# A cross-attention stream whose first chunk and queries are multiplied in unsplit fp32, with merged input transfers and unused products at the start

## The chip, the cores and the metric

The kernel runs on one core of a Trainium2 chip. The metric is the device time of one execution in microseconds. A core has five engines that run their own instruction queues and wait for each other through semaphores: TensorE (PE in the profile; its weight loads are PEld), VectorE (DVE), ScalarE (ACT), GpSimd (POOL) and SyncE (SP), which here issues the DMA transfers. All tiles lie in on-chip memory of 128 partitions; TensorE writes into accumulators (PSUM, here six banks of 128 x 512 for passing results and two that accumulate over the whole stream).

## The reference

The whole is one layer: cross-attention with a sigmoid in place of the softmax, then a causal attention block with rotary terms, then a mixture of 8 experts. What matters here is the first part. `x` has 256 rows of 512, the context 25088 rows of 512.

```
xn = layernorm(x)
qp = xn @ Wq.T + bq                  # 256 x 128
kp = ctx @ Wk.T + bk                 # 25088 x 128
vp = ctx @ Wv.T + bv                 # 25088 x 512
z  = sigmoid(qp @ kp.T / sqrt(128))  # 256 x 25088
x  = x + z @ vp
```

Then `x = x + attn(layernorm(x))` and `x = x + ffn(layernorm(x))`. All inputs are fp32.

## The kernel before

**Algebra and tiling.** The context is streamed once in 49 chunks of 512 keys. Each chunk comes twice from memory: transposed (`ctxT`, features on partitions, 1 MB) for the key product, and as it stands (`ctxN`, keys on partitions, 1 MB) for the weighted sum. The product with `Wv` is left to the tail: the stream accumulates `z @ ctx` in `acc[0]` and `acc[1]` (128 queries each) over all chunks, and the row sums of `z` in `zacc` for the bias.

**Split products.** A product of two fp32r tiles keeps fewer bits than one of plain fp32 tiles and takes less time (512 columns: 0.23 us from start to start at L88, against 0.87 us for the plain fp32 product at L522). To keep the bits all the same, an operand is split (`split`, L82): ACT casts it to fp32r (`hi`, L84), and DVE or POOL subtracts that from the source (`lo`, L85). `mm3` (L87) then issues three products, hi by hi, hi by lo and lo by hi (L88, L89, L90). In the tail, products that are few take both operands as plain fp32 in a single call.

**A chunk** `c` goes through these steps: `load_T` and `load_N` issue the transfers on SP; `split_T` and `split_N` split them; `kp_mm(c)` forms the keys (4 blocks of 3 products of 512 columns); `kp_out` adds the bias and splits the result (ACT L203, DVE L204); `scores` multiplies with `qp` (12 products of 256 columns a chunk), takes the sigmoid (ACT L212), adds `z` to `zacc` (DVE L214) and splits `z`; `av` accumulates (24 products of 512 columns). The loop at L288 works one chunk ahead: `kp_mm(c + 1)` stands ahead of the `av` products of chunk `c`, and `scores(c + 1, 0)` and `scores(c + 1, 1)` stand behind the `av` products of key tiles 1 and 2. The last two chunks' products for the second half of the queries are kept for the tail.

**The start** (L242 to L284) is what the change is about. SP issues, in this order, `wk` (256 KB), `x` in two halves, `wq`, chunk 0 of `ctxT` in four blocks, `bq` and `bk` as columns of 128 four-byte elements, chunk 1 of `ctxT` in two halves, chunks 0 and 1 of `ctxN`, and `bv`. ACT and POOL split `wk` and `wq`. DVE computes the moments of both halves of `x` (`moments`, L145, with the power -0.5 on POOL, L152) and normalizes (`normal`, L157). TensorE transposes the normalized halves (`transposed`, L162), and ACT and DVE split the transposed tile into `xh`, `xl`. Chunk 0 is split block by block, blocks 0 and 1 with DVE, 2 and 3 with POOL. TensorE's order is: two sets of transposes, `kp_mm(0)` blocks 0 and 1, the 12 products of the queries (L272), `kp_mm(0)` blocks 2 and 3, `kp_mm(1)` blocks 0 and 1, `scores(0, 0)`, `scores(0, 1)`, `kp_mm(1)` blocks 2 and 3, then the loop.

**What sets the order.** Each engine works through its instructions in the order in which the program issues them. Semaphores between engines follow from the tiles that are written and read; a tile of a tag with n buffers waits until the one n places before it is read to the end. DMA transfers share eight semaphores in turn, so a transfer may also wait for the one eight places before it. In the tail a written list (`ORDER`, L36) sets the order, step by step; step `N2v` (L654) writes the sum `x2` into the tiles in which `x` was.

Of the kernel before, what the change touches and what calls it, by code (L numbers as in the profile page):

```python
# [68 lines left out]
def body(ctx, tc, a, out, nch=NCH):  # L69
# [31 lines left out]
    def toks(t):  # L101
        return slice(t * P, (t + 1) * P)


    ident = sm.tile([P, P], F32, name="ident")
# [5 lines left out]
    x_sb = [sb.tile([P, D], F32, tag=f"x{t}", name=f"x_sb{t}") for t in range(2)]  # L111
    bq = sm.tile([P, 1], F32, name="bq")
    bk = sm.tile([P, 1], F32, name="bk")
# [92 lines left out]
    def scores(c, p):  # L206
# [7 lines left out]
        tt2(zacc, zacc, z, ALU.add)  # L214
        split(*zz[c, p], z)

# [20 lines left out]
    def load_split(n, tag):  # L237
        r = sb.tile([P, D], F32, tag="wr", name=f"{n}_r", bufs=2)
        nc.sync.dma_start(r, a[n])
        return r, pair(n, [P, D], tag)  # L240

    wk_r, wk = load_split("wk", "wk")  # L242
    for t in range(2):
        nc.sync.dma_start(x_sb[t], a["x"][:, t, :])
    wq_r, wq = load_split("wq", "at")
    load_T(0, 4)
    nc.sync.dma_start(bq, a["bq"])
    nc.sync.dma_start(bk, a["bk"])
    load_T(1, 2)
# [5 lines left out]
    xh, xl = pair("xa", [P, KD, T], "oh")  # L255
    warm = sm.tile([P, 1], F32, name="warm")
    nc.scalar.activation(warm, half, AF.Sigmoid)
    split(*wk, wk_r, nc.gpsimd)
    m = [moments(x_sb[tt], f"a{tt}") for tt in range(2)]
    xn = [normal(x_sb[tt], m[tt], f"xa{tt}") for tt in range(2)]  # L260
    split(*wq, wq_r, nc.gpsimd)
    xps = [transposed(bank(f"xa_ps{tt}"), xn[tt]) for tt in range(2)]
    for j in range(2):
        split_T(0, [j])
        split(xh[:, :, toks(j)], xl[:, :, toks(j)], xps[j])
    split_T(0, [2, 3], nc.gpsimd)
    load_T(2)
    kp_mm(0, [0, 1])
    qp = pair("qp", [P, T])
    ps = bank("qp_ps")[:, :T]  # L270
    for j in range(KD):
        mm3(ps, wq[0][:, toks(j)], wq[1][:, toks(j)], xh[:, j, :], xl[:, j, :], j == 0, j == KD - 1)  # L272
    kp_mm(0, [2, 3])
    split_T(1, [0, 1])
    split_T(1, [2, 3], nc.gpsimd)
    nc.scalar.activation(qp[0], ps, AF.Identity, bias=bq)
    nc.vector.scalar_tensor_tensor(qp[1], ps, bq, f(qp[0]), ALU.add, ALU.subtract)
    kp_out(0)
    split_N(0, [0, 1])
    kp_mm(1, [0, 1])  # L280
    scores(0, 0)
    scores(0, 1)
    split_N(0, [2, 3])
    kp_mm(1, [2, 3])  # L284

    per = -(-len(todo) // max(1, nch - 5))
    late = []
    for c in range(nch):  # L288
# [21 lines left out]
        if c < 2:  # L310
            split_N(c + 1)
        for t in range(NT):
            for q in now:
                av(c, t, q)
            if nx and t in (1, 2):
                scores(c + 1, t - 1)
# [8 lines left out]
    x2, xn, mo = [None] * 2, [None] * 2, [None] * 2  # L325
# [327 lines left out]
    @step  # L653
    def N2v(tt):  # L654
        x2[tt] = sb.tile([P, D], F32, tag=f"x{tt}", name=f"x2{tt}")
        tt2(x2[tt], ps_["wo", tt], x1[tt], ALU.add)
# [236 lines left out]
```

## Time and profile before

| what | value |
|---|---|
| three runs, median (lowest to highest) | 556.81 us (556.64 to 559.41) |
| profiled execution, its own time | 557.0 us |
| its span from the first to the last instruction | 555.2 us |
| busy share of the span: PE, DVE, ACT, POOL | 96%, 78%, 69%, 3% |
| mean granted clock of TensorE | 0.997 |
| data moved | 118.25 MB, mean 213 GB/s |

The page divides the span into 40 slices of 13.9 us. PE is at 9 tenths or more in nearly all of them; only the first slice (3 tenths) and the last one lie lower. A matmul's duration in the profile includes the time its result needs to come out, so that consecutive products overlap: what one costs in a run is the distance from start to start. A plain fp32 product appears as two records. Times are microseconds from the first instruction of the span.

### The profile page before, as it was taken

To read this page: it belongs to the slowest core of one execution; us is meant where nothing else is said; L and a number is where in the kernel's file an instruction comes from. 1 tells how busy PE (TensorE), PEld (TensorE's weight loads), DVE (VectorE), ACT (ScalarE), POOL (GpSimd) and SP (SyncE) were. 2 spreads that over 40 slices of the span, in tenths; PEclk is the share of its full clock that TensorE was granted. 3 is DMA by queue.
4 is the path that set the end of the run, shared out by engine and by line. 5 is a ranking of instruction groups with operands and counts; after the bars stand their busy time and mean duration, and the time that the engine had idled before them with its cause. 6 is when DMAs were issued, how large, how long until landed. Compare 5 with 4: busy or idle time off the path is not lost. (4 is left out here: it accounts for less than half of the span.)

```text
span 555.2 us, 7396 instructions
## 1 busy us (share of the span) xinstructions
PE 535.4 (96%) x2838; PEld 449.1 (81%) x2838; DVE 433.8 (78%) x471; ACT 381.4 (69%) x477; POOL 16.0 (3%) x25
## 2 busy tenths in 40 slices
PE   3999999999999999999999999999999999999984
PEld 3888888888888888888888888888888888887662
DVE  5899888887878787887878788787878788537853
ACT  5877787777676777667677777767677767528930
POOL 5200000000000000000000000000000000100000
PEclk9999999999999999999999999999999999999998
DMA  8997878774656647464655647475565747312001
GB/s 267 377 370 277 293 252 327 266 278 185 235 220 220 234 183 259 173 248 199 234 221 205 249 171 260 180 241 211 227 228 193 260 165 261 116 47 106 2 20 58
DMA packets 20644, 118.25 MB, mean 213 GB/s; under 512 B 2816, under 2 KB 3072, under 8 KB 7424
## 3 DMA queue, kind: packets, MB, share of 16 engines
q1 hardware_dynamic: 20608, 117.76, 58.6%
q8 instruction: 23, 0.38, 0.2%
q14 instruction: 13, 0.11, 0.0%
HBM read 115.13 MB, written 2.62 MB: 212 GB/s over the span
## 5 line engine op out<-in xcount | busy, mean ns | idle before, releaser
L85 DVE TENSOR_TENSOR N<-big,N 128x2048 fp32r<-128x2048 f32 (+1 forms) x53 | 112.1, 2119 | 57.7 <-ACT N L84 57.7
L88 PE MATMUL acc<-N,z 128*128 128x512 f32 x392 | 153.9, 393 | 0.0
L89 PE MATMUL acc<-N,z 128*128 128x512 f32 x392 | 153.7, 392 | 0.0
L90 PE MATMUL acc<-N,z 128*128 128x512 f32 x392 | 152.5, 389 | 0.0
L85 DVE TENSOR_TENSOR T<-big,T 128x2048 fp32r<-128x2048 f32 (+1 forms) x49 | 110.3, 2253 | 17.2 <-ACT T L84 17.2
L212 ACT ACTIVATE z<-sc 128x512 f32<-128x512 f32 x98 | 58.7, 599 | 78.8 <-PE sc L90 78.7
L84 ACT CAST N<-big 128x2048 fp32r<-128x2048 f32 (+1 forms) x55 | 94.4, 1725 | 6.2
L84 ACT CAST T<-big 128x2048 fp32r<-128x2048 f32 (+1 forms) x55 | 94.1, 1718 | 1.2 <-DMA big<-in_ctxT 1.2
L90 PEld LDWEIGHTS acc<-N,z 128*128 128x128 f32 x392 | 73.6, 188 | 16.1
L88 PEld LDWEIGHTS acc<-N,z 128*128 128x128 f32 x392 | 74.0, 189 | 12.3
L89 PEld LDWEIGHTS acc<-N,z 128*128 128x128 f32 x392 | 74.0, 189 | 11.7
L88 PE MATMUL kp_ps<-T,wk 128*128 128x512 f32 x196 | 76.9, 392 | 0.0
L90 PE MATMUL kp_ps<-T,wk 128*128 128x512 f32 x196 | 76.5, 390 | 0.0
L89 PE MATMUL kp_ps<-T,wk 128*128 128x512 f32 x192 | 74.7, 389 | 0.0
L214 DVE TENSOR_TENSOR zacc<-zacc,z 128x512 f32<-128x512 f32 x98 | 67.4, 688 | 6.9 <-ACT z L212 1.5
L85 DVE TENSOR_TENSOR z<-z,z 128x512 fp32r<-128x512 f32 x98 | 67.4, 688 | 0.0
L84 ACT CAST z<-z 128x512 fp32r<-128x512 f32 x98 | 61.0, 622 | 3.1
L203 ACT ACTIVATE kp<-kp_ps,bk 128x512 fp32r<-128x512 f32 x49 | 33.8, 691 | 39.8 <-PE kp_ps L90 39.8
L90 PE MATMUL sc<-qp,kp 128*128 128x256 f32 x196 | 55.8, 285 | 0.2 <-DVE kp L204 0.2
L89 PE MATMUL sc<-qp,kp 128*128 128x256 f32 x196 | 55.4, 283 | 0.0
L88 PE MATMUL sc<-qp,kp 128*128 128x256 f32 x196 | 54.9, 280 | 0.0
L88 PEld LDWEIGHTS kp_ps<-T,wk 128*128 128x128 f32 x196 | 37.1, 189 | 7.8
(174 smaller groups left out, 478.5 us busy)
## 6 DMA issues: line engine op xcount, KB each, us to landing
big<-in_ctxN SPq DMA_DIRECT2D x49, 1024.0 KB, 4.8
big<-in_ctxT SPq DMA_DIRECT2D x47, 1024.0 KB, 4.9
big<-in_gu SPq DMA_DIRECT2D x4, 1024.0 KB, 4.8
sp_wo<-w_wo SPq DMA_DIRECT2D x8, 256.0 KB, 4.4
wo<-sp_wo SPq DMA_DIRECT2D x2, 1024.0 KB, 6.1
big<-in_ctxT SPq DMA_DIRECT2D x4, 256.0 KB, 6.6
big<-in_ctxT SPq DMA_DIRECT2D x2, 512.0 KB, 6.3
r_wv<-in_wv SPq DMA_DIRECT2D x4, 256.0 KB, 6.6
```

The source lines that it names most:

```text
L84: copy(hi, src)
L85: eng.tensor_tensor(lo, src, f(hi), ALU.subtract)
L88: mm(ps, lhsT=ahi, rhs=bhi, start=first, stop=False)
L89: mm(ps, lhsT=ahi, rhs=blo, start=False, stop=False)
L90: mm(ps, lhsT=alo, rhs=bhi, start=False, stop=last)
L203: nc.scalar.activation(kp[c][0], ps, AF.Identity, bias=bk)
L212: nc.scalar.activation(z, ps, AF.Sigmoid, scale=1.0 / math.sqrt(128.0))
L214: tt2(zacc, zacc, z, ALU.add)
```

## The change

- `x` comes in one transfer into one tile of two halves; `x2` takes the same form in the tail.
- `bq` and `bk` come as two rows of 128 elements on ACT's queue, and two products with a one-element operand on TensorE turn them into two columns, which ACT copies from PSUM.
- Chunk 0 and chunk 1 of `ctxT` come in one transfer each; chunk 0 comes ahead of `wq`.
- Chunk 0 isn't split: `kp0(j)` multiplies `wk_r` with the arrived tile in plain fp32, four calls of 512 columns. The queries are formed from `wq_r` and the unsplit transposed `x` in four calls of 256 columns. `wq` is no longer split; `wk` still is, for the later chunks.
- `idle` issues products of a constant bf16 tile whose results nobody reads: five from the first microsecond on, and ten more behind the bias products.
- In the first chunks, more of the splits go to POOL, one block at a time; the order of the splits on ACT and DVE changes; `zacc` is added behind the split of `z` in chunk 0; and the scores of chunk 1 stand one key tile later among the products of chunk 0.

```
+    allb = sm.tile([P, P], BF16, name="allb")
+    nc.vector.memset(allb, 1.0)
...
-    x_sb = [sb.tile([P, D], F32, tag=f"x{t}", name=f"x_sb{t}") for t in range(2)]
-    bq = sm.tile([P, 1], F32, name="bq")
-    bk = sm.tile([P, 1], F32, name="bk")
+    x_all = sb.tile([P, 2, D], F32, tag="x", name="x_sb")
+    x_sb = [x_all[:, t, :] for t in range(2)]
+    brow = tmp("brow")[0:1, 0:2 * P].rearrange("p (i k) -> p i k", i=2)
+    bias = sm.tile([P, 2], F32, name="bias")
+    bq, bk = bias[:, 0:1], bias[:, 1:2]
...
-        tt2(zacc, zacc, z, ALU.add)
+        if c:
+            tt2(zacc, zacc, z, ALU.add)
         split(*zz[c, p], z)
+        if not c:
+            tt2(zacc, zacc, z, ALU.add)
...
-    def load_split(n, tag):
-        r = sb.tile([P, D], F32, tag="wr", name=f"{n}_r", bufs=2)
-        nc.sync.dma_start(r, a[n])
-        return r, pair(n, [P, D], tag)
-
-    wk_r, wk = load_split("wk", "wk")
-    for t in range(2):
-        nc.sync.dma_start(x_sb[t], a["x"][:, t, :])
-    wq_r, wq = load_split("wq", "at")
-    load_T(0, 4)
-    nc.sync.dma_start(bq, a["bq"])
-    nc.sync.dma_start(bk, a["bk"])
-    load_T(1, 2)
+    def idle(name, k):
+        ps = bank(name)
+        for _ in range(k):
+            mm(ps, lhsT=allb, rhs=allb[:, None, :].broadcast_to([P, 4, P]), start=True, stop=True)
+
+    wk_r, wq_r = (sb.tile([P, D], F32, tag="wr", name=f"{n}_r", bufs=2) for n in ("wk", "wq"))
+    nc.sync.dma_start(wk_r, a["wk"])
+    nc.sync.dma_start(x_all, a["x"])
+    load_T(0)
+    nc.sync.dma_start(wq_r, a["wq"])
+    for i, n in enumerate(("bq", "bk")):
+        nc.scalar.dma_start(brow[:, i, :], a[n].rearrange("p o -> o p"))
+    load_T(1)
     load_N(0)
     load_N(1)
     nc.sync.dma_start(bv, a["bv"])
...
-    xh, xl = pair("xa", [P, KD, T], "oh")
+    xa = sb.tile([P, KD, T], F32, tag="oh0", name="xa")
+    wk = pair("wk", [P, D])
     warm = sm.tile([P, 1], F32, name="warm")
     nc.scalar.activation(warm, half, AF.Sigmoid)
-    split(*wk, wk_r, nc.gpsimd)
+    idle("idlea", 5)
+    ps = bank("bias_ps")
+    for i in range(2):
+        mm(ps[:, i:i + 1], lhsT=brow[:, i, :], rhs=ones[0:1, :], start=True, stop=True)
+    copy(bias, ps[:, 0:2])
+    idle("idleb", 10)
+    kp[0] = bank("kp_ps0")
+
+    def kp0(j):
+        mm(kp[0], lhsT=wk_r[:, toks(j)], rhs=rT[0][:, j, :], start=j == 0, stop=j == KD - 1)
+
+    copy(wk[0], wk_r)
+    nc.gpsimd.tensor_tensor(wk[1], wk_r, f(wk[0]), ALU.subtract)
     m = [moments(x_sb[tt], f"a{tt}") for tt in range(2)]
     xn = [normal(x_sb[tt], m[tt], f"xa{tt}") for tt in range(2)]
-    split(*wq, wq_r, nc.gpsimd)
-    xps = [transposed(bank(f"xa_ps{tt}"), xn[tt]) for tt in range(2)]
-    for j in range(2):
-        split_T(0, [j])
-        split(xh[:, :, toks(j)], xl[:, :, toks(j)], xps[j])
-    split_T(0, [2, 3], nc.gpsimd)
+    xps = [transposed(bank("xa_ps0"), xn[0])]
+    kp0(0)
+    xps += [transposed(bank("xa_ps1"), xn[1])]
+    for j in range(1, KD):
+        kp0(j)
     load_T(2)
-    kp_mm(0, [0, 1])
+    copy(xa[:, :, toks(0)], xps[0])
+    vcopy(xa[:, :, toks(1)], xps[1])
+    split_T(1, [0, 1])
+    kp_out(0)
     qp = pair("qp", [P, T])
     ps = bank("qp_ps")[:, :T]
     for j in range(KD):
-        mm3(ps, wq[0][:, toks(j)], wq[1][:, toks(j)], xh[:, j, :], xl[:, j, :], j == 0, j == KD - 1)
-    kp_mm(0, [2, 3])
-    split_T(1, [0, 1])
-    split_T(1, [2, 3], nc.gpsimd)
+        mm(ps, lhsT=wq_r[:, toks(j)], rhs=xa[:, j, :], start=j == 0, stop=j == KD - 1)
+    split_T(1, [2])
+    kp_mm(1, [0, 1])
     nc.scalar.activation(qp[0], ps, AF.Identity, bias=bq)
     nc.vector.scalar_tensor_tensor(qp[1], ps, bq, f(qp[0]), ALU.add, ALU.subtract)
-    kp_out(0)
-    split_N(0, [0, 1])
-    kp_mm(1, [0, 1])
+    split_T(1, [3], nc.gpsimd)
+    split_N(0, [0])
+    split_N(0, [1], nc.gpsimd)
     scores(0, 0)
     scores(0, 1)
-    split_N(0, [2, 3])
     kp_mm(1, [2, 3])
+    split_N(0, [2])
+    split_N(0, [3], nc.gpsimd)
...
-        if c < 2:
-            split_N(c + 1)
+        if c == 0:
+            split_N(1, [0, 1])
+            split_N(1, [2, 3], nc.gpsimd)
+        if c == 1:
+            split_N(2)
         for t in range(NT):
             for q in now:
                 av(c, t, q)
-            if nx and t in (1, 2):
-                scores(c + 1, t - 1)
+            p = t - 1 - (c == 0)
+            if nx and p in (0, 1):
+                scores(c + 1, p)
...
-        x2[tt] = sb.tile([P, D], F32, tag=f"x{tt}", name=f"x2{tt}")
+        if tt == 0:
+            x2_all.append(sb.tile([P, 2, D], F32, tag="x", name="x2"))
+        x2[tt] = x2_all[0][:, tt, :]
```

More of the change, by code (lines that the diff above doesn't have):

```diff
@@ L324, in body @@
     x1 = [sb.tile([P, D], F32, name=f"x1{t}") for t in range(2)]
-    x2, xn, mo = [None] * 2, [None] * 2, [None] * 2
+    x2, xn, mo, x2_all = [None] * 2, [None] * 2, [None] * 2, []
     xT = [sb.tile([P, KD, P], F32, tag=f"xT{t}", name=f"xT{t}") for t in range(2)]
```

## The prediction

> **What bounds the kernel now.** I read four views: the page's busy rows, the table of busy time by stage, the order of time of the first 28 us, and the DMA issues. Stage table first; its columns are the stretch, its length, then busy us and count of PE, PEld, DVE, ACT and POOL, granted clock, DMA share, GB/s.
>
> ```profile
> PE 535.4 (96%) x2838; PEld 449.1 (81%) x2838; DVE 433.8 (78%) x471; ACT 381.4 (69%) x477; POOL 16.0 (3%) x25
> ...
> 0.00:7.63 7.63, 0.00 (x0) 0.00 (x1) 3.21 (x9) 2.36 (x4) 3.57 (x14) 1.00 0.73 199
> 7.63:15.73 8.10, 7.18 (x32) 6.03 (x33) 6.82 (x8) 6.16 (x12) 5.35 (x5) 1.00 0.96 367
> 15.73:27.49 11.76, 11.58 (x62) 9.71 (x60) 10.31 (x13) 10.88 (x15) 2.22 (x2) 1.00 0.90 370
> 27.49:461.31 433.82, 433.82 (x2162) 368.59 (x2160) 356.90 (x327) 312.62 (x325) 0.00 (x0) 1.00 0.65 235
> 461.31:555.20 93.89, 82.81 (x587) 64.81 (x585) 56.53 (x117) 49.42 (x124) 4.81 (x6) 0.98 0.22 79
> ```
>
> From 27.49, where chunk 2's key product starts, to 461.31 TensorE never rests: 45 chunks in 433.82 us, 9.64 each; DVE (82%), ACT (72%) and DMA (65%) have room. The diff touches nothing there that TensorE waits for, and the tail keeps its instructions. So the time changes by as much as the start of `kp_mm(2)` moves from 27.49, and everything is decided before it. There the order of time shows (start, duration, engine, line, what; in brackets the idle time and who ended it):
>
> ```profile
> 4.62 0.69 DVE L149 BATCH_NORM_STATS2 s6a<-x_sb 128x6 f32<-128x512 f32 x1 [3.01 <-DMA x_sb<-in_x]
> ...
> 6.02 0.69 DVE L149 BATCH_NORM_STATS2 s6a<-x_sb 128x6 f32<-128x512 f32 x1 [0.30 <-DMA x_sb<-in_x]
> ...
> 7.04 0.54 DVE L157 TENSOR_SCALAR xa<-x_sb,mva,rsa 128x512 f32<-128x512 f32 x1
> ...
> 7.63 1.12 PE L162 MATMUL xa_ps<-ident,xa 128*128 128x128 f32 x4 [7.63 <-DVE xa L157]
> ...
> 8.99 0.62 ACT L84 CAST T<-big 128x512 fp32r<-128x512 f32 x1 [1.01 <-DMA big<-in_ctxT]
> ...
> 11.43 0.63 PE L90 MATMUL kp_ps<-T,wk 128*128 128x512 f32 x1
> ...
> 11.86 0.63 PE L88 MATMUL kp_ps<-T,wk 128*128 128x512 f32 x1
> ...
> 13.71 1.15 ACT L84 CAST T<-big 128x512 fp32r<-128x512 f32 x2 [0.23 <-DMA big<-in_ctxT]
> ...
> 15.73 0.40 PE L88 MATMUL kp_ps<-T,wk 128*128 128x512 f32 x1
> ...
> 23.43 0.38 PE L90 MATMUL sc<-qp,kp 128*128 128x256 f32 x1 [0.18 <-DVE kp L204]
> ...
> 27.49 0.39 PE L88 MATMUL kp_ps<-T,wk 128*128 128x512 f32 x1
> ...
> 500.52 1.02 PE L522 MATMUL vs_ps<-wvu,ckv 128*128 128x512 f32 x2
> ```
>
> The reader is to see: x lands at 4.6 and 6.0, TensorE starts at 7.63 with transposes, and its products of 512 columns go every 0.43 us at 11.43 but every 0.2277 from 12.67 on (27.26 to 27.49). Chunk 1's first product goes at 15.73. From there to 27.49 stand 36 products of 512 columns (36 x 0.2277 = 8.20) and 24 of 256 (x 0.1175 = 2.82): 11.02 us of work in 11.76, so 0.74 us is stall, most of it at 23.43. The L522 row prices an unsplit fp32 product: two halves of 0.43 each, 0.87 for 512 columns; the eight products of 256 columns at L737 come every 0.43, and I use 0.44.
>
> **The change, part by part**, against the profiled execution: 557.0 us, 555.2 of span and 1.8 around it; 0.2 above the median of the three runs (556.81).
>
> *Transfers.* Before, pieces of 256 KB landed at 3.5 (wk), 4.6 and 6.0 (x), 7.3 (wq), 9.0, 9.6, 10.3, 11.0 (chunk 0), then chunk 1 at 13.7 and its values, 1 MB each, 2.5 us apart (16.2, 18.7). After, wk, x, chunk 0, wq, chunk 1 go in this order in whole pieces, and the 256 four-byte packets of bq and bk become two rows on ACT's queue. x: not before 3.5 + 1.27 (512 KB at the values' rate) = 4.7, not after 6.0, with as many bytes ahead as before; I take the middle, 5.4. Chunk 0: not before 4.7 + 2.5 = 7.2, not after 10.3, where as many bytes had landed; I take 8.5, nearer to the value row, since the 256 KB pieces from 9.0 on already came 0.65 apart. wq 9.6, chunk 1 at 12.1 (ends 10.5 and 13.6).
>
> [...]
>
> *Queries.* DVE's row for one half of x takes 1.10 us (4.62 to 5.72: statistics, aggregate, add), the second the same, and TensorE starts 0.6 after the first normalization starts (7.04 to 7.63): x + 1.1 + 1.0 + 0.6 = x + 2.7 = 8.1. That is 0.5 later than 7.63, since both halves now come together. The second half's normalization took 1.59 us beside POOL's split of wq; that split is gone, so it takes about 0.54 as the first did, done by 9.0.
>
> *TensorE to chunk 1.* Removed: 12 + 12 split products (12 x 0.2277 + 12 x 0.1175 = 4.1 warm, 1.2 more for the slow ones). Added: 4 x 0.87 + 4 x 0.44 = 5.2. With two sets of transposes (0.48 each by the late rows) it is 6.2 us in one run: 8.1 + 6.2 = 14.3 against 15.73, so the products that cost more pay by not waiting for splits. Chunk 0 is needed at 8.6; landing later than that, chunk 1 starts at landing + 5.7 (14.2 at 8.5).
>
> *Unused products.* Five from 1.3 on (0.43 each, to 3.5), then the two bias products, which wait for the bias rows, and ten more: 2.2 us at the fast pace, 4.3 at the slow. They end between 6 and 8.5 and push the transposes of 8.1 by 0 to 0.4; I take 0. The pace turned before 4.7 us after the first transposes (7.63 to about 12.4); counted from 1.3 that is 6.0, ahead of the queries. [...]
>
> *ACT, POOL, SP queues.* Two DMA issues (0.45 each by SP's rows) go ahead of ACT's table load, which ends at 3.0 instead of 2.0. Behind it wait the bias copy and wk's cast (4.6 instead of 3.49), then POOL's wk remainder (5.3 to 6.5) and, behind that on POOL, the power for x, ready at 6.5: nothing lost at x = 5.4, 0.3 at x = 4.7. SP has seven issues fewer ahead of the values, which only keeps its queue filled. Chunk 2's load waits for TensorE's last read of chunk 0 (12.5) instead of the splits (15.02) and lands near 20.4, before 21.9.
>
> *Splits of chunk 1.* After it lands: cast 0.61, two remainders 1.37, the remainder of kp 0.75, the third 0.69, that of qp 0.47: 3.9 us on DVE, so 16.0. The scores need it at 14.3 + 1.4 + 0.1 = 15.8: 0.2 to 0.3 lost. POOL takes three single pieces, 1.5 each by its rows (12.00, two in 2.99): ready at 17.0, 18.5, 21.7, used at 17.9, 19.8, 23.2; the cover is about 1 us each.
>
> *Scores of chunk 1 one tile later.* The remainder of kp is done at 22.0, the scores go at 22.6: the stall of 23.43 is gone. Next late is chunk 2's remainder on DVE, 24.9 against 25.6 needed. The zacc order and x's single tile cost nothing: same engine, same instructions, and in the tail the writer already stands behind the last reader.
>
> **Sum:** 14.3 + 0.3 + 11.0 = 25.6 for `kp_mm(2)`, 1.9 before 27.49; 557.0 - 1.9 = 555.1 us.
>
> **Rivals.**
> *Transfers no faster.* For it: all those bytes crossed by 10.3 and 13.6 before. Then chunk 1 starts at 10.3 + 5.7 = 16.0 and `kp_mm(2)` at 27.1: 556.6 us.
> *Transfers at full rate from wk on*, x at 4.4 to 4.7, chunk 0 by 7.2. For it: the value rows. Chunk 1 starts at 13.6, `kp_mm(2)` at 24.6: 554.1 us. Against it: DMA moved 199 GB/s in the first 7.63 us.
> *Pace not turned (the other side).* If the break for the bias rows, or TensorE's 1 us pause before the transposes, keeps the pace at 0.43, the 6.2 us cost up to 12.4: chunk 1 at 20.5, near 561 us. The change loses nothing until the pace turns after about 12.6 (chunk 1 at 16.6), and 0.5% only after about 18. Against it: in the rows of before, the pace turned with a pause of 0.92 us in between.
>
> **How the numbers follow.** Forecast (gains of 0.8 to 2.7) 0.53, transfers no faster 0.18, full rate 0.20, pace not turned 0.09. The 8 in 10 range cuts the outer part of the last two: 553.8 to 558.0. Half a per cent is 2.8 us, about what a measurement of this kernel tells from no change: faster by more, the full-rate case with what scatter adds, 0.20; slower by more, most of the pace case, 0.08; within, 0.72.
>
> **What would show it.** In the changed profile `kp_mm(2)` should start near 25.6, then 9.64 a chunk. Right steps: x ends DVE's wait at 5.4; chunk 0's fp32 products go 0.87 apart from 8.6; the first product of chunk 1 near 14.3; no gap near the scores of chunk 1. Wrong: fp32 products 1.7 apart; a DMA ending a wait of TensorE over 1 us; POOL's piece ending a TensorE wait after 17; a chunk period other than 9.64.

## The result and the profile after

| | before | after |
|---|---|---|
| median of 20 runs each (lowest to highest) | 558.84 us (556.64 to 561.47) | 558.09 us (557.07 to 560.97) |
| ratio after to before, 95% interval | | 0.9991, 0.9974 to 1.0008 |
| profiled execution, its own time; span | 557.0; 555.2 | 560.09; 558.3 |
| mean granted clock of TensorE in it | 0.997 | 0.989 |

The change makes no difference that can be measured. Before's three runs of the table above had a median of 556.81; its twenty have 558.84.

The table of busy time by stage, after (each row: stretch, length, then busy us and count of PE, PEld, DVE, ACT and POOL, granted clock, DMA share, GB/s):

```profile
0.00:7.75 7.75, 6.69 (x20) 2.89 (x21) 3.15 (x10) 2.16 (x4) 3.73 (x14) 1.00 0.73 258
7.75:14.27 6.52, 6.09 (x26) 3.74 (x24) 3.04 (x5) 2.92 (x5) 0.14 (x1) 1.00 1.00 419
14.27:26.92 12.65, 11.88 (x63) 9.61 (x62) 11.53 (x12) 11.08 (x18) 7.05 (x5) 1.00 0.91 350
26.92:461.06 434.14, 434.12 (x2162) 368.68 (x2161) 358.05 (x328) 313.15 (x325) 1.57 (x1) 1.00 0.65 234
461.06:558.30 97.24, 86.00 (x587) 66.58 (x585) 56.55 (x117) 49.36 (x124) 4.75 (x6) 0.94 0.21 76
```

Chunk 1 begins at 14.27, 1.46 earlier than before; chunk 2 (`kp_mm(2)`, the third stretch's end) at 26.92, only 0.57 earlier; chunk 4, at 46.54 against 46.79, only 0.25 earlier. POOL's busy time in the third stretch is 7.05 us; before it was 2.22 in the stretch from chunk 1 to chunk 2. The last stretch is 97.24 us long at a clock of 0.94, against 93.89 at 0.98. So the start gained 1.46, lost 1.2 of it again by chunk 4, and the tail, which the change leaves as it was, lost about 3 us in this execution. These are two matters, and both need their rows. (The trace's record of the granted clock begins only at 6.98; the unused products go 0.40 to 0.43 us apart ahead of it and 0.22 behind it, although the first row shows 1.00. In what follows, "the pace turns" means the beginning of that record.)

**The start**, in order of time (start, duration, engine, line, what; in brackets the idle time and who ended it):

```profile
1.06 2.31 PE L248 MATMUL idlea<-allb 128*128 128x512 bf16 x5 [1.06 <-DVE allb L106]
...
4.25 3.66 PE L248 MATMUL idleb<-allb 128*128 128x512 bf16 x10
4.92 0.69 DVE L153 BATCH_NORM_STATS2 s6a<-x_sb 128x6 f32<-128x512 f32 x1 [3.29 <-DMA x_sb<-in_x]
7.75 0.60 PE L166 MATMUL xa_ps<-ident,xa 128*128 128x128 f32 x4
8.78 1.10 PE L278 MATMUL kp_ps<-big,wk_r 128*128 128x512 f32 x2 [0.43 <-DMA big<-in_ctxT]
...
12.73 1.89 PE L297 MATMUL qp_ps<-xa,wq_r 128*128 128x256 f32 x8
14.27 0.59 PE L88 MATMUL kp_ps<-T,wk 128*128 128x512 f32 x1
...
22.83 0.50 PE L89 MATMUL acc<-N,z 128*128 128x512 f32 x1 [0.72 <-DVE N L85]
```

From the first unused product to 14.27 there is one wait, 0.43 us for chunk 0. The wait that matters is the last line: a product of values of chunk 0 (the chunk as it stands, `ctxN`) waits 0.72 us for the remainder of its block (`N`, the `lo` of the split, L85), and it is DVE that ends the wait, not POOL. From the start of the product before it that is 1.11 us instead of 0.23. A smaller wait of the same kind stands at 19.32, 0.44 instead of 0.23 behind the last start, for the remainder of `z`. Why DVE is late stands in its own rows beside POOL's, in the same view:

```profile
15.72 1.30 POOL L85 TENSOR_TENSOR T<-big,T 128x512 fp32r<-128x512 f32 x1 [7.83 <-ACT T L84]
...
16.19 1.37 DVE L85 TENSOR_TENSOR N<-big,N 128x512 fp32r<-128x512 f32 x1 [0.54 <-ACT N L84]
...
16.97 1.74 POOL L85 TENSOR_TENSOR N<-big,N 128x512 fp32r<-128x512 f32 x1
...
18.04 1.22 DVE L85 TENSOR_TENSOR z<-z,z 128x512 fp32r<-128x512 f32 x1 [0.47 <-ACT z L84]
...
20.28 1.35 POOL L85 TENSOR_TENSOR N<-big,N 128x512 fp32r<-128x512 f32 x1 [1.56 <-ACT N L84]
...
20.39 1.78 DVE L222 TENSOR_TENSOR zacc<-zacc,z 128x512 f32<-128x512 f32 x1
22.10 0.68 DVE L85 TENSOR_TENSOR N<-big,N 128x512 fp32r<-128x512 f32 x1
...
24.21 4.28 POOL L85 TENSOR_TENSOR N<-big,N 128x512 fp32r<-128x512 f32 x2 [2.59 <-ACT N L84]
...
25.56 3.48 DVE L85 TENSOR_TENSOR N<-big,N 128x512 fp32r<-128x512 f32 x2
```

A DVE subtraction or addition of 512 columns lasts 0.68 (the row at 22.10). Those that run while POOL works last 1.37, 1.22, 1.78. Add start and duration: POOL's pieces end at 17.02, 18.71 and 21.63; the DVE rows beside them end at 17.56, 19.26 and 22.17, each 0.54 or 0.55 later. So DVE's instruction doesn't seem to run more slowly all along; it seems to wait for POOL's to end. The waiting seems to go both ways: POOL's second piece, begun at 16.97 while DVE's row of 16.19 still ran, took 1.74 where the first took 1.30. At 24.21 POOL's two pieces end at 28.49 and DVE's second block at 29.04, 0.55 later again. So a piece that POOL takes from DVE is also taken out of DVE's time, and DVE is nearly full there (11.53 of 12.65 us in the third stretch).

The trace of before has the same pattern, in rows that the prediction read for another purpose or not at all:

```profile
8.02 1.59 DVE L157 TENSOR_SCALAR xa<-x_sb,mva,rsa 128x512 f32<-128x512 f32 x1 [0.45 <-POOL rsa L152]
...
8.06 1.27 POOL L85 TENSOR_TENSOR wq<-wq_r,wq 128x512 fp32r<-128x512 f32 x1
...
12.00 2.99 POOL L85 TENSOR_TENSOR N<-big,T 128x512 fp32r<-128x512 f32 x2 [2.67 <-ACT T L84]
...
12.99 2.55 DVE L85 TENSOR_TENSOR T<-big,T 128x512 fp32r<-128x512 f32 x2 [0.86 <-ACT T L84]
```

Two DVE blocks that take 1.28 together without POOL took 2.55 here and ended 0.55 after POOL's second piece (12.00 + 2.99 = 14.99; 12.99 + 2.55 = 15.54). The normalization of 8.02, of one tile and two columns, ended 0.28 after POOL's (9.61 against 9.33).

Not every DVE instruction is held. Before, POOL's next two pieces ran from 14.96 to 17.95. DVE's remainders of `qp` (15.46) and `kp` (16.65), which have one source in PSUM, took 0.47 and 0.75 beside them, and 0.48 and 0.74 in after with no POOL beside them (15.16 and 22.70). The next subtraction of two SBUF tiles, from 17.32, took 1.18 and ended at 18.50, 0.55 after POOL. Why the end lies 0.54 to 0.55 us behind POOL's, no trace or run here shows.

**The tail.** The same table of stages for the last 20 us, after:

```profile
538.12:542.87 4.75, 3.22 (x18) 2.40 (x17) 2.86 (x8) 0.86 (x2) 0.55 (x1) 1.00 0.08 30
542.87:549.70 6.83, 6.83 (x18) 4.08 (x18) 2.46 (x10) 0.00 (x0) 0.00 (x0) 0.50 0.21 77
549.70:553.11 3.41, 1.71 (x5) 0.43 (x3) 0.78 (x3) 0.54 (x2) 0.00 (x0) 1.00 0.00 0
553.11:558.30 5.19, 0.00 (x0) 0.00 (x0) 0.49 (x1) 0.00 (x0) 0.00 (x0) 0.50 0.17 58
```

and before, cut where its clock changed:

```profile
538.47:551.92 13.45, 8.56 (x37) 5.14 (x36) 6.58 (x21) 1.41 (x4) 0.55 (x1) 1.00 0.17 54
551.92:555.20 3.28, 0.00 (x0) 0.00 (x0) 0.00 (x0) 0.00 (x0) 0.00 (x0) 0.50 0.18 65
```

In after's execution the granted clock fell to 0.5 from 542.87 to 549.70, and TensorE's products there took nearly twice as long (the second gate and up products 3.62 us from 546.36, the first 1.99 from 538.12); in before's it fell only when TensorE had no more to do. That difference isn't the change's. In both kernels the runs lie in groups by mean granted clock: before, over the 106 runs that were taken beside the experiments, near 557.1 us at 0.997 to 0.998 (50 runs), 559 at 0.994 (22) and 561 at 0.990 (34); after, 557.8 (median of nine runs at 0.997) to 561.0. Taking the start of chunk 4 from the span in each profile makes the groups plain: from there to the end lie 508.4 us in before (555.23 - 46.79), and 508.4 to 508.7 in the eight other profiles in which the clock stayed full until the last products; 509.9 to 510.1 where the clock was at half for one step of 3.41 us; 511.5 to 511.8 where it was for two, as in after. So the time of a run is the start of chunk 4, plus 508.5, plus 0, 1.5 or 3.1 for the tail's clock, plus 1.8 around the span. For the rest of this document a kernel's start is read at chunk 4, and the tail apart.

### The profile page after: what moved, and what is told of

Its sections match the earlier page's. It is cut to its first block, busy times and chain, and to the rows that moved or that the text cites. A ratio compares the mean times of both kernels' runs of the same rounds, so it can differ in the third digit from the quotient of the medians.

```text
span 558.3 us, 7405 instructions
## 1 busy us (share of the span) xinstructions
PE 544.8 (98%) x2849; PEld 451.5 (81%) x2849; DVE 432.3 (77%) x469; ACT 378.7 (68%) x475; POOL 17.2 (3%) x25
## 5 line engine op out<-in xcount | busy, mean ns | idle before, releaser
L85 DVE TENSOR_TENSOR N<-big,N 128x2048 fp32r<-128x2048 f32 (+1 forms) x52 | 112.3, 2162 | 58.3 <-ACT N L84 58.3
L85 DVE TENSOR_TENSOR T<-big,T 128x2048 fp32r<-128x2048 f32 (+1 forms) x50 | 109.8, 2197 | 16.3 <-ACT T L84 16.2
L84 ACT CAST T<-big 128x2048 fp32r<-128x2048 f32 (+1 forms) x51 | 91.9, 1804 | 2.8 <-DMA big<-in_ctxT 2.8
L88 PE MATMUL kp_ps<-T,wk 128*128 128x512 f32 x192 | 74.9, 390 | 0.0
L90 PE MATMUL kp_ps<-T,wk 128*128 128x512 f32 x192 | 74.8, 390 | 0.0
L89 PE MATMUL kp_ps<-T,wk 128*128 128x512 f32 x192 | 74.8, 389 | 0.0
L219 DVE TENSOR_TENSOR zacc<-zacc,z 128x512 f32<-128x512 f32 x96 | 66.0, 688 | 6.8 <-ACT z L216 1.5
L85 DVE TENSOR_TENSOR z<-z,z 128x512 fp32r<-128x512 f32 x98 | 68.0, 694 | 0.5 <-ACT z L84 0.5
L207 ACT ACTIVATE kp<-kp_ps,bias 128x512 fp32r<-128x512 f32 x49 | 33.8, 690 | 38.4 <-PE kp_ps L90 38.4
```

Of the source, the lines that this page charges most:

```text
L84: copy(hi, src)
L85: eng.tensor_tensor(lo, src, f(hi), ALU.subtract)
L88: mm(ps, lhsT=ahi, rhs=bhi, start=first, stop=False)
L89: mm(ps, lhsT=ahi, rhs=blo, start=False, stop=False)
L90: mm(ps, lhsT=alo, rhs=bhi, start=False, stop=last)
L207: nc.scalar.activation(kp[c][0], ps, AF.Identity, bias=bk)
```

## The experiments

They were taken in four sets, each on one chip with the kernel before beside it; the medians of before were 557.61, 559.12, 558.43 and 559.08 in the four sets (29, 35, 29 and 13 runs). Nothing of the layer's computation is left out in any of them.

| kernel | chunk 1 starts | chunk 4 starts | from there to the end | median us (runs) | ratio to before, 95% |
|---|---|---|---|---|---|
| before | 15.73 | 46.79 | 508.4 | 558.84 (20) | |
| after | 14.27 | 46.54 | 511.8 | 558.09 (20) | 0.9974 to 1.0008 |
| values on DVE | 15.37 | 45.99 | 510.1 | 557.97 (12) | 0.9965 to 1.0015 |
| no unused products | 16.64 | 48.93 | 511.7 | 561.88 (6) | 1.0049 to 1.0098 |
| before, unused products | 14.85 | 46.71 | 511.5 | 557.97 (12) | 0.9970 to 1.0013 |
| before, tail filled | | 46.94 | 508.4 | 558.42 (12) | 0.9981 to 1.0022 |
| after, transfers cut | 14.37 | 46.64 | 508.4 | 557.41 (12) | 0.9950 to 0.9999 |
| cut, values on DVE | 13.65 | 45.57 | 509.9 | 557.14 (12) | 0.9939 to 0.9989 |
| the same, tail filled | 13.88 | 45.89 | 508.5 | 556.02 (12) | 0.9928 to 0.9972 |
| after, once more | 15.19 | 47.49 | 508.7 | 558.09 (12) | 0.9964 to 1.0011 |
| late values | 14.66 | 47.38 | 508.5 | 556.82 (12) | 0.9935 to 0.9981 |
| chunk 0 split | 13.82 | 44.80 | 508.5 | 555.42 (12) | 0.9915 to 0.9962 |
| late values, bias late | 13.56 | 48.64 | 508.5 | 556.92 (12) | 0.9942 to 0.9984 |
| chunk 0 split, bias late | 13.99 | 45.66 | 508.5 | 555.85 (10) | 0.9918 to 0.9967 |

The columns of starts are one execution each, the profiled one; medians are of all runs.

### Is it POOL? Values of chunks 0 and 1 on DVE

```
-    split_N(0, [1], nc.gpsimd)
+    split_N(0, [1])
...
-    split_N(0, [3], nc.gpsimd)
+    split_N(0, [3])
...
-            split_N(1, [2, 3], nc.gpsimd)
+            split_N(1, [2, 3])
```

> The changed kernel, with the six blocks of the values of chunks 0 and 1 that it gives to POOL subtracted on DVE instead. Contention theory: in the changed kernel DVE's rows of 0.69 us stretch to 1.2 to 1.8 while POOL subtracts, so the third block of chunk 0's values is ready at 22.78 and TensorE waits 0.72 there and 0.3 one chunk later. Without POOL these rows keep 0.69, the wait of 0.72 falls under 0.3, kp_mm(2) starts near 25.9 (26.92 in the changed kernel) and kp_mm(4) near 45.2 (46.54): 1.0 to 1.3 us less. Rival (DVE has no room for the added work): the six blocks add 4.1 us to DVE, the waits stay or grow, kp_mm(4) at 46.5 or later. Either way the tail keeps its scatter, so the time shows it only within about 1 us.

The edit moves four blocks, two of each chunk (the expectation says six). DVE has more instructions and each is short, in the order of time of that kernel:

```profile
19.19 0.68 DVE L85 TENSOR_TENSOR z<-z,z 128x512 fp32r<-128x512 f32 x1
...
20.99 0.68 DVE L222 TENSOR_TENSOR zacc<-zacc,z 128x512 f32<-128x512 f32 x1
21.59 1.28 DVE L85 TENSOR_TENSOR N<-big,N 128x512 fp32r<-128x512 f32 x2
...
25.92 2.49 DVE L85 TENSOR_TENSOR N<-big,N 128x512 fp32r<-128x512 f32 x4
```

Four blocks of chunk 1's values take 2.49 us; after, DVE's two took 3.48 beside POOL's two. From chunk 1's first product to `kp_mm(2)` it is 11.27 us instead of 12.65, with no wait of TensorE on DVE or POOL left in its rows from 9 to 38 us. The next chunk's period is 9.67. A late start of chunk 1 (15.37) isn't what makes these distances short: the second profile of the change (below) starts it at 15.19 and needs 12.63 and 10.03. The start of chunk 4 came only 0.55 earlier than after's, and not the 1.3 that was expected, since chunk 0 landed at 9.74 in this execution and TensorE waited 1.24 for it. In the median there is little (557.97 against 558.09); among runs of like clock there is more: the three at 0.997 took 555.1, 555.24 and 556.09 against a median of 557.81 for after and 557.16 for before beside it, and the four at 0.989 to 0.990 took 558.8 to 559.4 against 560.1 and 561.0 for after. POOL's share in the values is the cause of what was lost between chunk 1 and chunk 3, and the scatter that hides it lies elsewhere.

### Are the unused products needed? Without them, and before with them

```
-    idle("idlea", 5)
...
-    idle("idleb", 10)
```

> The changed kernel without its fifteen unused products. If they are what brings TensorE to its fast pace in time, then the fp32 products of chunk 0 go 1.7 us apart instead of 0.87 at least for the first, the pace turns between 11 and 15.6, the first product of chunk 1 starts at 15.5 to 17.3 instead of 14.27, and kp_mm(4) starts 0.5 to 2.5 later than 46.54, less where DVE is behind anyway. Rival (the pace turns through the transposes and fp32 products themselves): first product of chunk 1 within 0.3 of 14.27 and no change of kp_mm(4).

```profile
7.82 1.11 PE L166 MATMUL xa_ps<-ident,xa 128*128 128x128 f32 x4 [3.86 <-DVE xa L161]
9.66 2.04 PE L276 MATMUL kp_ps<-big,wk_r 128*128 128x512 f32 x2 [0.72 <-DMA big<-in_ctxT]
11.49 1.06 PE L166 MATMUL xa_ps<-ident,xa 128*128 128x128 f32 x4
```

The first unsplit product takes 2.04 here instead of 1.10, and the pace turns at 12.7. Chunk 4 starts at 48.93, 2.4 after the change with them (0.9 of it from a later landing of chunk 0), and the median is 561.88. This is the only one of the experiments that is measurably slower than before: without the unused products, the rest of the change costs more than it saves.

The same fifteen products put at the head of the kernel before, where the operands stay split:

```
+    allb = sm.tile([P, P], BF16, name="allb")
+    nc.vector.memset(allb, 1.0)
...
+    ips = bank("idlea")
+    for _ in range(15):
+        mm(ips, lhsT=allb, rhs=allb[:, None, :].broadcast_to([P, 4, P]), start=True, stop=True)
     split(*wk, wk_r, nc.gpsimd)
```

> The kernel before with fifteen unused products in front of its first transposes and nothing else of the change. Theory that the splits limit the start of before: the pace turns by about 7 instead of 12.6 and the first products go 0.23 apart, but chunk 0's last two blocks are subtracted on POOL until 15.0 (rows at 12.00, 2.99 for two), so the first product of chunk 1 comes no earlier than 15.4 (15.73 before) and kp_mm(4) moves by less than 0.4 from 46.79. Rival (the slow pace limits the start of before): six products at 0.43 become six at 0.23, 1.2 to 1.5 us less at kp_mm(4).

The pace turned at 4.0 and chunk 1 started at 14.85 instead of 15.73, but its second half started at 18.74 (18.75 before) and chunk 4 at 46.71 (46.79): the early start was lost again at the splits, where TensorE waited 0.5 us at 16.40. In before the pace isn't what limits; in after it is, as the two profiles of the change will show.

### Is the transfer's size worth something? Chunks 0 and 1 cut as before

```
-    load_T(0)
+    load_T(0, 4)
...
-    load_T(1)
+    load_T(1, 2)
```

> The changed kernel with chunk 0 in four transfers and chunk 1 in two, as before; x stays in one. In the four executions of kernels with whole pieces chunk 0 landed at 8.6 to 9.7 and its first product waited up to 1.2 us for it. Theory: in pieces the first product needs only 256 KB and goes right behind the first transposes (near 8.5), the first product of chunk 1 stays at 14.0 to 14.4 however late the last piece lands; but POOL's contention with DVE remains, so kp_mm(4) stays at 46.3 to 46.8 (46.54 in the changed kernel). Rival (merging is worth something by itself): the last piece lands over 0.5 later than 9.7 and the first product of chunk 1 comes after 14.8.

The pieces of chunk 0 landed at 7.66, 8.44, 9.11 and 9.77, the first product ran at 8.96, chunk 1 started at 14.37 and chunk 4 at 46.64, 0.1 from after; the wait of 0.7 for `N` is there as before. The median is 557.41. Merging these transfers gains nothing in this kernel, and among runs of like clock it loses: the six at 0.997 have a median of 557.04, against 557.95 for the seven of the change itself beside it (below). What a whole transfer does have is scatter: as one transfer, chunk 0 landed at 8.64, 9.74, 9.52 and 7.35 in four profiles, and in the three in which TensorE waited for it, its first product came 0.14 us behind the landing (8.78, 9.88 and 9.66); cut, its last piece came between 8.59 and 10.20 in the profiles of after's order, and its first one at 6.5 to 7.7. One thing speaks for whole transfers: chunk 2 landed at 18.7 to 20.2 in those four profiles, and at 20.6 to 21.6 in the seven with cut ones. Here nothing waits long for it; in later kernels it decides.

### How much does the change itself scatter? The change once more

> The changed kernel as it is, for a second trace of its start and its times beside the others on one chip. Expected: kp_mm(4) at 46.5 plus what chunk 0 lands later than 8.64; the runs 557 to 561 with a median within 0.7 us of the kernel before; in the runs with the highest granted clock 2 to 2.6 us slower than the kernel with the values on DVE (555.1 to 556.1).

```profile
4.25 4.45 PE L248 MATMUL idleb<-allb 128*128 128x512 bf16 x10
8.49 1.06 PE L166 MATMUL xa_ps<-ident,xa 128*128 128x128 f32 x4
9.34 1.45 PE L278 MATMUL kp_ps<-big,wk_r 128*128 128x512 f32 x2
```

All ten unused products went at the slow pace here (4.45 us against 3.66); they held the transposes up to 8.49, although chunk 0 had landed at 7.35, and the pace turned only at 10.2, in the middle of the first real products. Chunk 4 started at 47.49, 0.95 later than in the first execution. Yet this execution took 557.95 us against 560.09, since its tail stayed at full clock. The median is again 558.09, and the wait of 0.7 us for `N` is there again. So the loss at DVE belongs to the kernel, and the tail's 3 us to the execution; and the late turn of the pace went through to chunk 4 in full.

### Is it the tail that scatters? Unused products among the last steps

Twelve products without a reader (`WMp`, a step that the program already has) are set into the written list where TensorE waits, first in the kernel before, and then in the change with cut transfers and the values on DVE:

```
- GUp:0 N2g:1 ... ITp:0 ITc:0:v ... GUp:1 OUs:0 ... ITp:1 ITc:1:a
+ GUp:0 WMp:0:5 N2g:1 ... ITp:0 WMp:1:2 ITc:0:v ... GUp:1 WMp:2:4 OUs:0 ... ITp:1 WMp:3:1 ITc:1:a
```

> The kernel before with twelve unused products of the bf16 mask in four gaps of the tail (5 behind the first gate and up products, 2 ahead of the second logits, 4 behind the second gate and up products, 1 ahead of the last product). Clock theory: the scatter of 556.6 to 561.5 comes from TensorE's granted clock falling to a half in the tail (in the changed kernel's execution at 542.9, which made the second gate and up products 3.62 instead of 1.99 long); with the gaps filled it does not fall before the last products, the runs lie within about 1 us of each other and their median 1.5 to 2 us under that of the kernel before. Rival (the scatter comes from the start or from memory): the scatter stays, the median within 0.5 us, or up to 1 us longer for the added products.

The runs near 561 at 0.990 are gone (none of 12, against 7 of 29 of before beside it), but the median is not lower: 558.42, against 557.61. Five runs at 0.997 or 0.998 lie from 556.6 to 557.2, three at 0.999 at 558.4, and four at 0.993 or 0.994 from 558.5 to 559.3. So of the expectation only the end of the slowest runs held; for the median its rival was right (up to 1 us longer), and what scatters besides the tail wasn't found in this kernel. Over the six kernels with a filled tail in the table, none of 70 runs lies at 0.992 or below; of before's 106 runs 34 do.

> The changed kernel with both: the values of chunks 0 and 1 subtracted on DVE, and chunk 0 in four, chunk 1 in two transfers. Theory: the two losses add, so the first product of chunk 1 starts at 14.0 to 14.6 (15.37 with the values on DVE alone, where chunk 0 landed at 9.74) and kp_mm(4) at 45.1 to 45.6 (45.99 there). Rival (DVE is full from 17 on, so an earlier start is given back): kp_mm(4) at 45.9 or later.

> The kernel of the run with both, and the twelve unused products in the tail. If the head is as there and the tail's pace falls less often, the runs lie between 554 and 558 with a median of 555.5 or less, 2 us or more under that of the kernel before. Rival (the tail's products cost what they save): the median equals that of the run with both within 0.5 us.

The first joins the cut transfers and the values on DVE, the second fills the tail as well. The first starts chunk 1 at 13.65 and chunk 4 at 45.57, and TensorE still waits 0.3 us for DVE's remainder of `z`. Chunk 4 is within what was expected, but from chunk 1 on it takes 31.9 us where the kernel with the values on DVE alone took 30.6: most of the early start is given back. Its median is 557.14 with 3.8 us from lowest to highest; with the tail filled, 556.02 (555.5 or less was expected) with 2.3, and eleven of twelve runs at 0.997 or above. The stages of the filled tail, cut where the clock changed:

```profile
537.56:553.69 16.13, 11.06 (x49) 6.16 (x48) 6.58 (x21) 1.41 (x4) 0.55 (x1) 1.00 0.18 60
553.69:554.40 0.71, 0.00 (x0) 0.00 (x0) 0.00 (x0) 0.00 (x0) 0.00 (x0) 0.50 0.00 0
```

### What is late next? Values of chunk 1 behind its scores

In the kernel with cut transfers, values on DVE and a filled tail, the period from chunk 2 to chunk 3 is still 10.64 (36.25 - 25.61) instead of 9.64. One theory was that DVE does the values of chunk 1 too early, ahead of the remainder of `z`:

```
-            split_N(1, [2, 3])
...
                 scores(c + 1, p)
+                if c == 0:
+                    split_N(1, [2 + p])
```

> The kernel with both edits and the tail's products, and the last two blocks of chunk 1's values split behind the scores of chunk 1 instead of ahead of them. Theory: there the wait of 1.0 us in chunk 2 (10.64 from kp_mm(2) to kp_mm(3) instead of 9.64) comes from DVE, whose remainder of z stands behind four blocks of values; with two of them behind it that distance falls to 9.65 to 9.95, kp_mm(4) starts at 44.9 to 45.3 (45.89 there) and the median falls by 0.5 to 0.9 from 556.0. Rival (the total of DVE's work is the limit): the wait moves one chunk on and kp_mm(4) stays at 45.6 to 45.9.

The period became 9.65, and one chunk later TensorE waited 1.9 us; the waits of that kernel (engine, line, who ended it: us, times, longest):

```profile
PE sc L90 <- DVE kp L208: 1.9, 1, 1.9
```

Chunk 4 started at 47.38, 1.5 later than without the edit, and the median rose by 0.8. The work was put off and the queue with it: DVE had no slack to catch up. The rival's mechanism held, the wait moved one chunk on, though chunk 4 came later than it said.

### Are the unsplit products worth it? Chunk 0 split again

The kernel with cut transfers, values on DVE and a filled tail, with chunk 0 split and multiplied in three products as before:

```
     def kp0(j):
-        mm(kp[0], lhsT=wk_r[:, toks(j)], rhs=rT[0][:, j, :], start=j == 0, stop=j == KD - 1)
+        split_T(0, [j])
+        kp_mm(0, [j])
```

> The kernel with both edits and the tail's products, with chunk 0 split in four blocks and multiplied in three products a block again (ACT and DVE alone); the queries stay unsplit. It undoes the half of the fp32 part that concerns the keys. Theory from the prediction (unsplit products cost TensorE 0.8 more and pay by sparing DVE 2.8 and ACT 2.4 us): first product of chunk 1 within 0.5 of 13.9, but DVE's chain for the scores of chunk 0 ends near 16.0 to 16.5 instead of 15.7, kp_mm(4) 0.3 to 1.0 later than 45.89, median 556.2 to 557.0. Rival (the unsplit form is what the change lives on): kp_mm(4) 1.5 or more later. Second rival (it costs more than it saves): kp_mm(4) earlier than 45.6.

```profile
9.21 0.50 PE L89 MATMUL kp_ps<-N,wk 128*128 128x512 f32 x1 [0.49 <-DVE N L85]
...
13.82 0.58 PE L88 MATMUL kp_ps<-T,wk 128*128 128x512 f32 x1
...
44.80 0.39 PE L88 MATMUL kp_ps<-T,wk 128*128 128x512 f32 x1
```

Chunk 1 starts at 13.82, as with the unsplit products (13.88), although TensorE waits 0.49 for the first split: twelve split products take 12 x 0.23 = 2.7 us where four unsplit ones take 4 x 0.87 = 3.5. Chunk 4 starts at 44.80, 1.1 earlier than without the edit and 2.0 earlier than before, and the median is 555.42, the lowest here.

The 1.1 us can't be put down to the edit. They go with the landing of chunk 2: at 20.58 in this execution and at 21.58 in that of the kernel without the edit, where already the first piece of chunk 0 had come 0.7 later (7.23 against 6.51). In both, chunk 2 landed 2.5 us behind the transfer ahead of it. ACT waits for chunk 2, DVE for ACT, and TensorE, in the kernel without the edit, for DVE:

```profile
21.73 1.91 ACT L84 CAST T<-big 128x2048 fp32r<-128x2048 f32 x1 [0.72 <-DMA big<-in_ctxT]
...
23.67 2.29 DVE L85 TENSOR_TENSOR T<-big,T 128x2048 fp32r<-128x2048 f32 x1 [1.04 <-ACT T L84]
...
29.63 0.50 PE L90 MATMUL acc<-N,z 128*128 128x512 f32 x1 [0.37 <-DVE z L85]
```

and with it:

```profile
20.66 1.91 ACT L84 CAST T<-big 128x2048 fp32r<-128x2048 f32 x1 [0.34 <-DMA big<-in_ctxT]
...
22.61 2.29 DVE L85 TENSOR_TENSOR T<-big,T 128x2048 fp32r<-128x2048 f32 x1 [0.61 <-ACT T L84]
```

In the four kernels with cut transfers and all of these values on DVE in their first order, chunk 4 starts 24.2 to 24.3 us after chunk 2 lands, with chunk 1 starting at 13.65 to 13.99 in no order of its own. What is left for the edit is the medians of twelve runs each, 555.42 against 556.02, from two sets. So the unsplit product of the keys gains nothing here; whether it costs up to 0.6 us isn't shown. A kernel with whole transfers, these values on DVE and a filled tail wasn't run.

### When does the pace turn? The bias products later

In after's rows the two bias products, with one column each, stand between the first five unused products and the other ten. The edit, made first in the kernel with late values and then in the one with chunk 0 split, gives twelve, the bias products, and four, and sets the bias copy behind `wk`'s cast on ACT:

```
-    idle("idlea", 5)
+    idle("idlea", 12)
...
-    copy(bias, ps[:, 0:2])
-    idle("idleb", 10)
+    idle("idleb", 4)
...
     copy(wk[0], wk_r)
+    copy(bias, ps[:, 0:2])
```

The expectations speak of windows and of steps of 3.41 us. Of these the traces show that the record of the granted clock changes after whole steps of 3.413 us: it begins at 6.98 in after and changes first at 542.87, 535.89 us or 157 steps later; in before it begins at 12.61 and changes at 551.92, 539.31 us or 158 steps later. That TensorE has to be busy without a break for one such step is the author's theory.

> The kernel with the late values, and the bias products behind twelve unused products, with four more behind them; ACT casts wk ahead of the bias copy. Theory: in the second trace of the change the pace turned only at 10.2 (6.98 in the first) because the wait for the bias rows and their four tiny products (3.31 to 4.25) break the busy stretch; without the break it turns at 8.0 at the latest, wherever its windows fall, and the first product of chunk 1 starts by 14.2. Rival (the turn does not depend on the break): turns later than 8.5 remain possible; nothing else changes, median within 0.4 of the kernel with the late values.

> The kernel in which chunk 0 is split again, POOL is out, the transfers are cut and the tail is filled (555.42 us median), and beside these the bias products stand behind twelve unused products instead of five, four follow, and the bias copy stands behind wk's cast on ACT. Theory, that the pace turns when TensorE is busy without a break for one of the 3.41 us steps: the turn comes before 6.9 us (7.24 before this edit, 5.87 in the other kernel with it), the four unused products end before the transposes, and since chunk 0's products wait for their splits (0.5 us at 9.2) most of the gain is lost there: the fifth chunk's key product starts at 44.5 to 44.8 instead of 44.80, median 555.0 to 555.5, with fewer runs above 556. Rival, that the turn was never late in this kernel and that the landing of chunk 0 alone sets its start: the same start to 0.2 us either way, median within 0.3 us of 555.42. Third, that wk's cast, moved ahead, is no earlier since it waits for the transfer, and the bias copy now late holds up the queries: start above 45.2, median above 556.

The pace turned at 5.87 and 6.81, and chunk 1 of the first started at 13.56, 1.1 before the same kernel without the edit. Over all eight profiles with five unused products ahead of the bias products the turn lay between 6.98 and 10.2. This agrees with the theory that the bias products break up a busy stretch, but two traces, one of them only 0.17 below the others, don't prove it. Neither kernel is faster for it: 556.92 against 556.82, and 555.85 against 555.42. In the last kernel chunk 4 started at 45.66, 0.86 later than in the one without the edit, with chunk 2 landing 0.85 later (21.43 against 20.58) and DVE busy for all of 25 to 30 us; so by then it is the transfers and DVE that decide, not TensorE's pace. In the first of the two, after a wait of 1.9 us as in the kernel without the edit, the clock fell for one step in mid-stream, which it had not done there:

```profile
43.42:46.83 3.41, 3.41 (x12) 2.83 (x12) 3.41 (x4) 1.22 (x2) 0.00 (x0) 0.50 0.82 300
```

## Why the prediction was right or wrong

The forecast was 555.1 us and "within half a per cent" the likeliest outcome. The median is 558.09: the outcome is the one given most chance, but the time is 3.0 us above the forecast and 0.09 above the end of the range. That the outcome came true is in part luck: the start lost most of its gain, and before's own time, 556.81 in the three runs that the sum started from, is 558.84 over twenty. Step by step:

*x at 5.4, transposes at x + 2.7.* Right: x ended DVE's wait at 4.92, within the bounds and 0.5 earlier than taken, and 4.92 + 2.7 = 7.6 against 7.75. *Chunk 0 at 8.5, wq 9.6, chunk 1 at 12.1:* they landed at 8.64, 9.31 and 11.79. *Chunk 1's first product at 14.3:* 14.27. The two records of an unsplit product came 0.43 apart, as priced. But one execution is not the kernel: in two profiles of the change, and two more with the same transfers and unused products or without these, chunk 0 landed anywhere from 7.35 to 9.74. The case "transfers at full rate" (chunk 0 by 7.2) very nearly came about in the second profile and gained nothing, since the unused products stood in front of the transposes until 8.49.

*Chunk 0 at 8.5, needed at 8.6.* The sum has no wait for it. As one transfer chunk 0 held up its first product by 0.43 us in one execution, not at all in another, by 1.24 and 0.72 in two experiments with the same transfers. Cutting it and chunk 1 again moved chunk 1 by 0.1 against the first profile and by 0.8 against the second, and runs of like clock got 0.9 faster. So the price of the whole transfer is below the 2.0 us that lay between before's first and last piece (9.0 and 11.0), but it isn't nothing, and the merging gains nothing in return here.

*Unused products push the transposes by 0 to 0.4; the pace turns at 6.0.* A step that failed, worth 0.9 us in one profile of two. The turn came at 6.98 and 10.2, 1.0 and 4.2 later than taken. The price for the transposes was 0.15 in the first execution (7.75 against 4.9 + 2.7) and 0.95 in the second (8.49 against 4.84 + 2.7), and there the first real products went at the slow pace besides: chunk 1 at 15.19. The sum counted busy time from 1.3 although the bias products cut the busy stretch in two; that this break made the turn late fits the two kernels without it but isn't proved. The rival "pace not turned" named just this break, and half of it occurred: the pace turned, but late.

*"POOL takes three single pieces, 1.5 each by its rows ...; the cover is about 1 us each."* This is the main step that failed, worth 1.7 us in both profiles. The cover was reckoned for POOL's own results alone, and the price to DVE was put at nothing. The pieces took 1.3 to 1.7, as priced, and were ready at 17.0, 18.7 and 21.6, as forecast; what they did was to stretch DVE's rows beside them from 0.68 to 1.2 to 1.8. TensorE waited 0.7 us for DVE at 22.83, and the next chunk's period, with POOL's last two pieces in it, was 9.98 instead of 9.64. The 11.0 us from chunk 1 to `kp_mm(2)`, plus 0.3, became 12.65 (12.63 in the second profile), and 11.27 and 9.67 with POOL's values taken back to DVE: the sum was right for that kernel. It was right only as long as chunk 2 lands early enough: 20.4 was forecast, 19.85 and 18.67 came, but with the transfers cut it was 20.6 to 21.6, and then 11.3 to 11.7 and 10.1 to 10.6 even without POOL. The prediction had the row of it in hand, 1.59 us for the second normalization "beside POOL's split of wq", used it to claim a gain where POOL's work went away, and didn't ask where POOL's work was added.

*"The products that cost more pay by not waiting for splits."* Not borne out once the other limits are gone: with chunk 0 split again, chunk 1 started at the same time (13.82 against 13.88), and the median didn't rise. The comparison was made with the kernel before, in which the splits were late for other reasons.

*Everything is decided before `kp_mm(2)`; from there 9.64 a chunk.* Nearly right: one chunk later another 0.34 was lost, and from `kp_mm(3)` (36.90) it is 9.64 in both. `kp_mm(2)` should have started at 25.6; it did at 26.92. A small misreading: of before's 0.74 us of stall, put down to 23.43 for the most part, the rows show 0.34 there (0.46 instead of 0.12 from start to start).

*The tail keeps its instructions.* It does, and even so took 3.3 us more in after's execution, where the granted clock fell. The prediction set its sum against one execution without such a fall (557.0) and the median of three (556.81), while before's medians over the larger sets are 557.61 to 559.12, and its range contained nothing for a tail that loses 3 us.

How the miss of 3.0 us divides: by the sum of the result's section, after's first start with a tail at full clock would be 46.54 + 508.5 + 1.8 = 556.8 and its second 557.8, which is also the median of its runs at 0.997 (557.81). The forecast's own start, 25.6 and two periods of 9.64, gives 44.9 + 508.5 + 1.8 = 555.2. So 1.7 to 2.6 us are the start (1.7 of them DVE beside POOL, the rest the late turn), and the other 0.4 to 1.3 are the tail's clock. Where the tail stays at full clock, after is even 0.7 slower than before (557.8 against 557.1), and that its median is nonetheless 0.75 lower is due to the groups: two of its 20 runs lie above 560, of before's 20 six. Whether the change has a part in that or chance alone isn't shown.

## What to carry to other kernels

Where two engines share work, price the piece on both: here every subtraction given to POOL also held up the DVE subtraction or addition beside it, to 0.54 or 0.55 us behind its own end, and the trace of before had rows that said so. A gain at the start is only worth what the next engine in line leaves of it; after TensorE was freed here, DVE and the landing of chunk 2 decided, and no help from POOL was better than its help. Before a difference between two profiles is put down to an edit, look at what landed when: here 1.0 of 1.1 us went with a transfer that came earlier. Before a sum is set against a time, look at how the runs of the kernel lie by granted clock: a fall of it in the tail cost up to 3.1 us here, more than the 1.9 that the whole change was to win, and twelve products without a reader took its largest steps away.

## What the runs showed of the hardware that was not expected

- DVE's additions and subtractions of two SBUF tiles end 0.54 to 0.55 us after the POOL subtraction beside them, in four places of after and two of before; the rows are longer by it, up to 1.78 instead of 0.68. Two rows of before with a source in PSUM, 0.47 and 0.75 long, aren't.
- The granted clock falls for 3.41 us or for twice that (543.47 to 546.88 with the values on DVE, 542.87 to 549.70 in after, 43.42 to 46.83 with late values and bias late). One such step in the tail costs 1.5 us, two cost 3.1. The first change of the record comes a whole number of such steps after its beginning, 157 in after and 158 in before. What decides a fall isn't TensorE's busy share in the step before as the profile has it: 2.33 of 3.41 us were followed by one (values on DVE, 540.06 to 543.47), 2.18 in the kernel before (545.08 to 548.50) were not. This stays open.
- One transfer of 1 MB in the first 10 us landed at 7.35 to 9.74 from one profile to another, while chunk 0 in four pieces had its first piece by 6.5 to 7.7 and its last by 8.6 to 10.2.
